# Summing four more steps of an attention pass as A (E - 1) g, with the rows of exp(0.2 s) made by ScalarE

## The chip, the core and the metric

The kernel runs on one core of a Trainium2 chip. The metric is the device time of one execution in microseconds (us); lower is better. The kernel before takes 2042.51 us in the median of three runs (2039.18 to 2042.93).

## What is computed

Two graph layers over 4096 nodes with 512 features, all in fp32. The adjacency A is a 4096 x 4096 matrix of zeros and ones, about 0.8% of it ones. Layer 0 has eight heads of 64 features:

```python
feats = einsum('nf,hfo->hno', X, W)
s_self = einsum('hno,ho->hn', feats, a_self)
s_neigh = einsum('hno,ho->hn', feats, a_neigh)
dense = s_self[:, :, None] + s_neigh[:, None, :]
dense = where(dense > 0, dense, 0.2 * dense)      # leaky
dense = dense * A[None, :, :]
attn = softmax(dense, axis=-1)                    # over all 4096, zeros too
out = einsum('hij,hjo->hio', attn, feats) + b
x = layernorm(x + relu(out))
```

Layer 1 is an attention within 32 graphs of 128 nodes each: query, key and value are x times Wq, Wk, Wv plus biases; the score within a graph is query · key · scale plus twice A; a softmax times the values is added to x and normalised. A second, general path in the file handles other inputs and does not run here.

## The kernel before

**Layer 0 without a score matrix.** exp of the leaky score is the larger of exp(s_self + s_neigh) and exp(0.2 (s_self + s_neigh)). Each of these is a product of something of the row i and something of the column j. So the kernel keeps, for each node and head, exponentials as columns (`d_all`, `e_all`, `e_b`) and as rows in DRAM (`pu_d`: rows p, u, and for some heads U = 1/u), and one VectorE operation makes a tile of weights: `q = max(p_row, d_j) * A` (L1534). ScalarE, and for every eighth tile VectorE, makes from `q` a mark of one byte that says which branch won (L1544, L1539); the marks summed by TensorE (`dens`, L1597) give the softmax's denominators.

**Passes, chunks, cycles, steps.** The heads are taken in four passes r of two heads. Each pass goes through four chunks c of 1024 nodes i, each chunk through 32 steps j of 128 neighbours. Passes 0 to 2 group eight steps to a cycle (`wide=8`), pass 3 four. TensorE's order is the program's (its schedule is written out by hand); the other engines' and the DMA queues' order is set by a scheduler at build time, except where `keep_in_program_order` pins an instruction. A step is:

- `accf += A f` with f split in two parts: four matmuls (L1558), which need no `q`;
- two `q`, one for each head, and their marks;
- `acc += q g`: eight matmuls of 32 columns, recorded as sixteen (L1581).

A cycle runs, on TensorE: L1558 of its steps, small pieces of other work, L1581 of its steps, then `dens` for eight steps. The chunk ends with `ys = (accf + S_col) * u_row + acc` on VectorE (L1278, L1286), whose transposes and denominators follow as pieces in later cycles.

**Folded steps.** Some steps are folded: VectorE makes `max(p_row, d_j) * U_row` (L1522) and then `(q - c_j) * A` (L1525), that is A (E - 1) g up to row and column factors; its L1581 matmuls go to `accf`, and the four L1558 matmuls of the step fall away. It needs the rows `U_row` (two of 512 KB) and the column `c_all`. Passes 0 and 3 have folded steps: pass 0 has j = 10, 18 in chunk 0 and j = 2, 10, 18 in the others; pass 3 has 6, 7 and 7 in chunks 1 to 3.

**Pass 0 has more to do.** It reads A itself as blocks of 1024 x 512 through the GpSimd queue (`a_b`, L605, three buffers, loaded ten steps ahead), turns them on TensorE (L617), casts them on ScalarE to `at` (L628), and stores `at` to DRAM (`at_d`, L629) for the later passes, which load it back (L635). It also sums the columns of exponentials over A (`ae`, L1479).

**Loads at SP.** At the start of each chunk: `p_row` (L1434, two of 512 KB, two buffers each) and `u_row` (L1440, two of 256 KB, one buffer). In each cycle: `f_s` (L1496, 512 KB for four steps) and `g_s` (L1501). `U_row` (L1462) goes into a buffer `ck` in pass 0. From pass 1 on, blocks `ck` of A are loaded and checked by ScalarE (L1249, L1250).

**Other work in pass 1.** `weights_of_layer_1` (L1018) is a generator. Each `yield` names a cost, and a cycle runs pieces until a credit of 6.0 is used up; pieces that end a chunk come first. It loads weights q, k and v (L1038), forms M = Wq^T Wk (L1043), turns v (L1055, L1056) and forms the bias terms with `partial_sums` (L572). M falls into the second to fourth cycle of chunk 2.

**Setup** (the first 160 us) forms the features (L818), and for each block k of four tiles the exponentials on ScalarE (L750, L751, L754); `rows_of_exponentials` (L778) takes reciprocals on VectorE (L780), turns them (L786), copies (L793) and stores the rows.

**Layer 1** (`layer_1`, L1088) runs its eight blocks as pieces in pass 3 and after it, with `values` (L1186, L1194) and `rows_out` (L1200, L1202).

Of the kernel before, what the change touches and what calls it, by code (L numbers as in the profile page):

```python
# [19 lines left out]
P = 128  # L20
# [384 lines left out]
def adjacency_streamed_path(  # L405
# [57 lines left out]
    f_d = dram.tile([PR, NT // 4, P, 4 * 2 * FP], F32, name="f_d")  # L463
    FOLDED = (0, PR - 1)
    FOLDS = {4: (1,), 5: (0, 1), 6: (0, 1, 2)}, {2: (1,), 4: (1,), 5: (0, 1), 6: (0, 1, 2)}
    HU = 2 * len(FOLDED)
    pu_d = dram.tile([2 * H + HU, N], F32, name="pu_d")
    at_d = dram.tile([NCH, NT, P, C], F32, name="at_d")
# [17 lines left out]
    for c in range(FC):  # L486
# [11 lines left out]
    nb_all = const.tile([P, NT, H], F32, name="nb_all")  # L498
    c_all = {
        r: (const if r else early).tile([P, NT, 2], F32, name="c_all") for r in FOLDED  # L500
    }
    below_0 = const.tile([P, 1], F32, name="below_0")
# [46 lines left out]
    def misc(shape, dtype=F32):  # L549

        banks.append(banks.pop(0))
        return banks[-1].tile(shape, dtype, name="ps_m")
# [86 lines left out]
    with tc.tile_pool(name="setup1", bufs=1, side="right") as one, tc.tile_pool(  # L639
# [60 lines left out]
        for c in range(FC // 2):  # L700
            score_columns(c, False)
        powers = one.tile([P, 5, H], F32, name="powers")
        for i, v in enumerate((ALPHA, 1.0, ALPHA - 1.0, 1.0 - ALPHA, -ALPHA)):
            nc.vector.memset(powers[:, i, :], v)
# [32 lines left out]
        def exponentials(k, u, sc):  # L737

            j = 4 * k + u
            if u == 0:  # L740
                pu_js[k] = two.tile([P, 4, 2 * H + HU], F32, name="pu_j")
            st = small.tile([P, 5, H], F32, name="st")
            for lo, hi, w in ((0, 3, 1), (3, 5, 0)):
                ends_of_setup["DVE", u] = nc.vector.tensor_tensor(
                    st[:, lo:hi].rearrange("p k (q h) -> p k q h", q=2),
                    sc[:, None, :, :, w].to_broadcast([P, hi - lo, 2, H // 2]),
                    powers[:, lo:hi].rearrange("p k (q h) -> p k q h", q=2),
                    OP.mult,
                )
            nc.scalar.activation(e_all[:, j], st[:, 0:2], AF.Exp)  # L750
            nc.scalar.activation(  # L751
                pu_js[k][:, u, : 2 * H].rearrange("p (k h) -> p k h", k=2), st[:, 3:5], AF.Exp
            )
            nc.scalar.activation(d_all[:, j, :], st[:, 2], AF.Exp)  # L754

        def parts_of_exponentials(k):
# [3 lines left out]
            )  # L760
            for r in FOLDED:
                nc.vector.reciprocal(
                    c_all[r][:, blk], e_all[:, blk, 1, 2 * r : 2 * r + 2]
                )
            eb = e_b[:, blk]
# [12 lines left out]
        def rows_of_exponentials(k):  # L778
            for i, r in enumerate(FOLDED):
                nc.vector.reciprocal(  # L780
                    pu_js[k][:, :, 2 * H + 2 * i : 2 * H + 2 * i + 2],
                    pu_js[k][:, :, H + 2 * r : H + 2 * r + 2],
                )
            pr = pss.tile([2 * H + HU, 4, P], F32, name="ps_set")
            for u in range(4):
                nc.tensor.transpose(pr[:, u, :], pu_js[k][:, u], ident)  # L786
            if k < NB - 1:
                row = late.tile([2 * H + HU, 4 * P], F32, name="pu_row")
            else:
                row = hp_.tile([P, CT, FP], F32, name="hst")  # L790
                row = row.rearrange("p t n -> p (t n)")[: 2 * H + HU, : 4 * P]
            rows[k] = row
            ends_of_setup["ROW"] = nc.scalar.copy(  # L793
                row.rearrange("p (q n k) -> p q k n", q=2, k=2),
                pr.rearrange("p (q k) n -> p q k n", q=2),
            )
            nc.gpsimd.dma_start(pu_d[:, ts(k, 4 * P)], row)
# [220 lines left out]
    def weights_of_layer_1(keep, wp):  # L1018
# [15 lines left out]
        ws = {}  # L1034
        for name, w in (("q", Wq), ("k", Wk), ("v", Wv)):
            yield 6.0
            ws[name] = wp.tile([P, FC, F], F32, name="w_" + name)
            nc.sync.dma_start(ws[name], w.rearrange("(c p) f -> p c f", p=P))  # L1038
        yield 6.0
        for m in range(FC):  # L1040
# [10 lines left out]
            yield 3.7  # L1051
        for o in range(FC):
            pv = misc([P, FC, P])
            for k in range(FC):
                nc.tensor.transpose(pv[:, k, :], ws["v"][:, o, ts(k, P)], ident)  # L1055
            nc.scalar.copy(L1["wvT"][:, :, ts(o, P)], pv)  # L1056
            if o % 2:
                yield 1.3

        pc = misc([P, 1])  # L1060
        kb = wp.tile([P, FC, P], F32, name="kb")
        nc.vector.tensor_copy(kb, cols["k"][:, :, None].to_broadcast([P, FC, P]))
# [5 lines left out]

        qb = ws["v"][:, 2, :P].rearrange("p (c n) -> p c n", c=FC)
        nc.vector.tensor_copy(qb, cols["q"][:, :, None].to_broadcast([P, FC, 32]))  # L1070
        pick = ws["v"][:, 3, :P]
        nc.vector.tensor_copy(pick, pick_col.to_broadcast([P, P]))
        parts = []
        for i, (wide, rhs) in enumerate(((kb, ws["q"]), (qb, ws["k"]))):
            pu = misc([P, F])
            partial_sums(pu, wide, rhs)
            parts.append(ws["v"][:, i, :])
            nc.scalar.mul(parts[i], pu, scale)
        yield 6.0
# [5 lines left out]
        nc.scalar.copy(L1["zb"], pz)  # L1085
        yield 2.0

    def layer_1(blk, x1b, lp, lp1, lp2):  # L1088
# [93 lines left out]

        def values(u):
            pv = misc([P, F])
            for f in range(FC):
                nc.tensor.matmul(  # L1186
# [5 lines left out]
                )  # L1192
            vs[u] = lp.tile([P, F], F32, name="v_t")
            nc.vector.tensor_add(vs[u], pv, L1["bv"])  # L1194

# [26 lines left out]
        values(2)  # L1222
        values(3)
        yield
        if blk == NT // 4 - 1:
            rows_out((2,))
            rows_out((3,))
        else:
            rows_out((2, 3))
        yield  # L1230
# [193 lines left out]
    steps = [(r, c, j) for r in range(PR) for c in range(NCH) for j in range(NT)]  # L1424

    def main_pass(r, ae=None, wide=4):

        for c in range(NCH):
            p_row = []
            for h in range(2):  # L1430
                p_row.append(rowp.tile([P, C], F32, name=f"p_row{h}"))
                in_order(
                    r == 0 and c < 2,
                    nc.sync.dma_start(p_row[h], broadcast_rows(pu_d[2 * r + h, ts(c, C)], P, C)),  # L1434
                )
            u_row = urowp.tile([P, C], F32, name="u_row")
            for h in range(2):
                in_order(
                    r == 0 and c < 2,
                    nc.sync.dma_start(  # L1440
                        u_row[h * FH : (h + 1) * FH, :],
                        broadcast_rows(pu_d[H + 2 * r + h, ts(c, C)], FH, C),
                    ),
                )
            U_row = []

            def folded(j):

                if r == PR - 1:
                    return r in FOLDED and c > 0 and j % 4 in FOLDS[c > 1].get(j // 4, ())  # L1450
                return r in FOLDED and j % 8 == 2 and (0 if c else 8) < j < NT - 8

            def rows_for_folded():

                for h in range(2):
                    if r == PR - 1:
                        pool, shape, name = ((hp_, [P, CT, FP], "hst"), (pools.get("lp1"), [P, C], "U_row"))[h]
                    else:
                        pool, shape, name = ckp, [P, CK], "ck"
# [3 lines left out]
                        U_row[h],  # L1463
                        broadcast_rows(pu_d[2 * H + 2 * FOLDED.index(r) + h, ts(c, C)], P, C),
                    )
# [24 lines left out]
            for j0 in range(0, NT, wide):  # L1490
# [3 lines left out]
                for k in range(j0 // 4, (j0 + wide) // 4):  # L1494
                    f_s[k] = fsp.tile([P, 4, 2, FP], F32R, name="f_s")
                    ins = nc.sync.dma_start(  # L1496
                        f_s[k].rearrange("p u s n -> p (u s n)").bitcast(F32), f_d[r, k]
                    )
# [4 lines left out]
                    )  # L1503
                    in_order(r == 0 and c == 0 and j0 < 16, ins)
                if at_step == 0:
                    cast_steps(0, 6, last_pair)
                if any(map(folded, range(NT))) and j0 == (4 if r else 0):
                    rows_for_folded()
# [126 lines left out]
    banks.extend([ctx.enter_context(tc.tile_pool(name="ps_misc2", bufs=2, space=PSUM))] * 2)  # L1635
    with tc.tile_pool(name="wl1", bufs=1, side="right") as wp:
        work.append(weights_of_layer_1(keep, wp))
        work.append(kind_of_graphs(wp))
# [69 lines left out]
```

## Time and profile before

| | us |
|---|---|
| runs, median (lowest to highest) | 2042.51 (2039.18 to 2042.93) |
| profiled execution, its own time | 2043.19 |
| its span, first to last instruction | 2041.3 |
| setup | 0 to 160.2 |
| pass 0 | 160.2 to 583.0 |
| pass 1 | 583.0 to 979.9 |
| pass 2 | 979.9 to 1355.5 |
| pass 3, with layer 1 beside it from its second chunk | 1355.5 to about 1902 |
| rest of layer 1 | to 2041.3 |

The stages are cut where TensorE starts the first L1558 matmul of a pass. A line of the profile's groups gives the line of the kernel, engine, operation, output and inputs, count, busy time and mean duration, and then the engine's idle time just before these instructions and what ended it. TensorE's recorded matmuls overlap, so their mean (594 ns for L1581) is longer than the distance between them; busy times of a group are the time covered. The granted TensorE clock is given as a share of full speed, the DMA share as the mean busy share of 16 engines (it can exceed 1, since packets overlap). Moved data is 558.7 MB, 274 GB/s in the mean.

### The profile page before, as it was taken

What the parts mean: (1) busy time and instruction counts of PE and PEld (TensorE: products, weight loads), DVE (VectorE), ACT (ScalarE), POOL (GpSimd) and SP (SyncE); (2) the same over time, 40 slices, a digit from 0 to 9 for tenths busy, and PEclk for the clock granted to TensorE, in tenths of its full rate; (3) what the DMA queues carried; (4) which work ended last, traced back from release to release, by engine and by line L of the source; (5) the groups of instructions that cost most, each with busy time, mean ns of one, the idle gap of its engine ahead of it and who ended that gap; (6) DMA issues with size and microseconds to landing.
All of it is one profiled execution on the core that took longest, in us unless ns stands there. A gap on an engine that the chain in (4) does not pass through costs nothing.

```text
span 2041.3 us, 38200 instructions
## 1 busy us (share of the span) xinstructions
PE 2005.9 (98%) x14981; PEld 1030.0 (50%) x14981; DVE 1744.8 (85%) x2219; ACT 1533.1 (75%) x1872; POOL 231.0 (11%) x362
## 2 busy tenths in 40 slices
PE   8999999999999999999999999999999999999997
PEld 7885545444444444444444544444444444445443
DVE  5668898898999998798999989999997897889754
ACT  3348988788888889788899889999786566567420
POOL 1222222222200000000000000000020210211111
PEclk9999999999999999999999999999999999999999
DMA  6899999999999999788999999989975775775211
GB/s 206 240 320 280 283 286 288 285 280 282 316 377 342 346 359 342 261 311 292 318 321 338 313 328 338 335 277 368 323 277 186 249 255 173 232 273 176 73 55 44
DMA packets 209386, 558.70 MB, mean 274 GB/s; under 512 B 25052, under 2 KB 66012, under 8 KB 209196
## 3 DMA queue, kind: packets, MB, share of 16 engines
q1 hardware_dynamic: 144844, 433.65, 61.0%
q0 software_dynamic: 62272, 121.98, 23.3%
q8 instruction: 120, 1.97, 0.4%
q10 hardware_dynamic: 2080, 0.52, 0.1%
q14 instruction: 70, 0.57, 0.1%
HBM read 499.13 MB, written 107.28 MB: 297 GB/s over the span
## 4 chain that ended last, share of the span: by engine, by line
PE 85%; DMA 7%; DVE 5%; issue 1%; ACT 1%; SPq 0%; POOL 0%; POOLq 0%; DVEq 0%; ACTq 0%
PE acc L1581 35%; PE accf L1558 20%; PE ps_fe L818 5%; PE ps_m L1186 5%; PE ps_m L1114 5%; PE dens L1597 5%; DMA a_b<-in_adj_dram 4%; DVE q L1534 3%; PE accf L1581 2%; PE ps_m L1141 1%; PE ps_m L1200 1%; DMA hp_l<-hs_d 1%; PE ps_m L617 1%; DMA at_d<-at 1%; PE ps_m L1043 1%
## 5 line engine op out<-in xcount | busy, mean ns | idle before, releaser
L1534 DVE SCALAR_TENSOR_TENSOR q<-p_row,d_all,at 128x1024 f32<-128x1024 f32 x962 | 1168.1, 1279 | 106.0 <-PE acc L1581 78.8
L1544 ACT ACTIVATE mark<-q,nb_all 128x1024 fp8e4<-128x1024 f32 x834 | 926.8, 1144 | 174.7 <-DVE q L1534 160.1
L1581 PE MATMUL acc<-q,g_s 128*32 128x512 f32 x7696 | 853.7, 594 | 1.1 <-DVE q L1534 0.4
L1581 PEld LDWEIGHTS acc<-q,g_s 128*32 128x32 f32 x7696 | 250.2, 110 | 557.2 <-issue 496.3
L1558 PE MATMUL accf<-at,f_s 128*128 128x512 f32 x1924 | 469.3, 400 | 1.7 <-ACT at L628 1.6
L1558 PEld LDWEIGHTS accf<-at,f_s 128*128 128x128 f32 x1924 | 357.2, 189 | 107.3 <-issue 27.8
L1249 ACT ACTIVATE ck<-ck,neg_half_f 128x1024 f32<-128x1024 f32 x128 | 146.0, 1141 | 28.5 <-DMA ck<-in_adj_dram 28.4
L1250 ACT ACTIVATE ck<-ck,neg_quarter 128x1024 f32<-128x1024 f32 x128 | 146.3, 1143 | 1.8
L1597 PE MATMUL dens<-mark,e_b 128*6 128x512 fp8e4 x2048 | 125.3, 379 | 2.5 <-DVE mark L1539 2.5
L818 PE MATMUL ps_fe<-w_sb_f,xT_f 128*128 128x264 f32 (+1 forms) x512 | 121.6, 395 | 1.7 <-ACT xT_f L730 1.7
L628 ACT CAST at<-ps_m 128x1024 fp32r<-128x1024 fp8e4 x124 | 116.3, 1022 | 4.8 <-issue 2.0
L1186 PE MATMUL ps_m<-wvT,x1T 128*128 128x512 f32 x256 | 114.2, 594 | 0.0
L1114 PE MATMUL ps_m<-x1T,M_sb 128*128 128x512 f32 x256 | 113.1, 595 | 0.0
L818 PEld LDWEIGHTS ps_fe<-w_sb_f,xT_f 128*128 128x128 f32 x512 | 100.5, 200 | 16.2 <-ACT xT_f L730 2.3
L1372 POOL DMA_DIRECT2D hs_d<-hst x12 | 10.7, 896 | 828.1 <-DVE hst L1362 817.5
L1539 DVE TENSOR_SCALAR mark<-q,d_all 128x1024 fp8e4<-128x1024 f32 x128 | 96.2, 751 | 4.7
L629 POOL DMA_DIRECT2D at_d<-at x128 | 69.1, 540 | 272.5 <-ACT at L628 94.0
L1597 PEld LDWEIGHTS <-e_b 128*6 128x6 bf16 x2048 | 55.9, 86 | 80.1 <-issue 38.2
L1529 ACT ACTIVATE mark<-q,below 128x1024 fp8e4<-128x1024 f32 x62 | 69.6, 1153 | 24.5 <-DVE q L1525 24.2
L1114 PEld LDWEIGHTS ps_m<-x1T,M_sb 128*128 128x128 f32 x256 | 48.0, 190 | 58.9 <-issue 57.1
L1525 DVE SCALAR_TENSOR_TENSOR q<-q,c_all,at 128x1024 f32<-128x1024 f32 x62 | 77.3, 1273 | 0.0
L1186 PEld LDWEIGHTS ps_m<-wvT,x1T 128*128 128x128 f32 x256 | 47.7, 190 | 56.3 <-issue 55.1
(207 smaller groups left out, 1294.9 us busy)
## 6 DMA issues: line engine op xcount, KB each, us to landing
at<-at_d SPq DMA_DIRECT2D x384, 512.0 KB, 6.1
f_s<-f_d SPq DMA_DIRECT2D x128, 512.0 KB, 7.8
at_d<-at POOLq DMA_DIRECT2D x128, 512.0 KB, 19.1
ck<-in_adj_dram SPq DMA_DIRECT2D x128, 512.0 KB, 5.5
g_s<-g_d SPq DMA_DIRECT2D x128, 256.0 KB, 5.9
f_d<-fst POOLq DMA_DIRECT2D x16, 1024.0 KB, 7.5
a_b<-in_adj_dram POOLq DMA_DIRECT2D x32, 512.0 KB, 21.7
p_row<-pu_d SPq DMA_DIRECT2D x32, 512.0 KB, 6.7
```

The costliest lines, as they stand in the source:

```text
L628: ends_of_setup["ACT"] = nc.scalar.copy(at, both[:, :, k])
L818: nc.tensor.matmul(pf[:, q, :, cols], tile_j(xTs[k][:, c].rearrange("p u n -> p (u n)"), u), w_sb[:, c, 4 * q : 4 * q + 4, cols], start=(c ...
L1114: nc.tensor.matmul(pz, L1["M"][:, f, ts(c, P)], x1T[:, f, :], start=(f == 0), stop=(f == FC - 1),)
L1186: nc.tensor.matmul(pv, x1T[:, f, ts(u, P)], L1["wvT"][:, f, :], start=(f == 0), stop=(f == FC - 1),)
L1249: tc.keep_in_program_order(nc.scalar.activation(ck, ck, AF.Square, bias=neg_half))
L1250: nc.scalar.activation(ck, ck, AF.Abs, bias=neg_quarter, accum_out=binp[:, k : k + 1])
L1534: ends_of_setup["Q"] = nc.vector.scalar_tensor_tensor(q, p_row[h], d_j, ats[r, c, j].bitcast(F32), op0=OP.max, op1=OP.mult)
L1539: nc.vector.tensor_scalar(mark, q, d_j, None, op0=OP.is_gt, saturate=False)
L1544: nc.scalar.activation(mark, q, AF.Sigmoid, bias=nb_all[:, j, hh : hh + 1], scale=BIG, saturate=False,)
L1558: nc.tensor.matmul(accf[:, s, :], f_s[j // 4][:, j % 4, w, :], ats[r, c, j][:, ts(s, HB)], start=(j == 0 and w == 0), stop=(j == NT - 1 an ...
L1581: nc.tensor.matmul(dst[o : o + 32, s, :], g_s[j // 4][:, j % 4, h, o % FH : o % FH + 32], qs[j, h][:, ts(s, HB)], start=(j == 0), stop=(j ...
L1597: nc.tensor.matmul(dens[lo : lo + 6, :], e_b[:, j, 2 * r + h, :], marks[j, h][:, ts(s, HB)], start=(j == 0), stop=(j == NT - 1),)
```

## The change

- ScalarE now makes the rows exp(0.2 s) directly, for all eight heads, beside the other two rows; the reciprocals L780 go, and `pu_d` has 24 rows and not 20. `c_all` is computed in setup for pass 0 alone; for passes 1 and 3 three VectorE operations at the pass's start add up the parts in `e_b` and take the reciprocal. These tiles lie in the pools `wl1` and `lp1`.
- Pass 0 folds j = 8, 16, 24 of every chunk. Pass 1 folds j = 8, 16, 24, 25 of chunk 2. Pass 3 folds the same steps as before.
- `f_s` loads only the steps from the first to the last that are not folded.
- In pass 0, `u_row` is loaded in the chunk's second cycle (chunk 0: at its start) and the next chunk's `p_row` in the third, both pinned.
- Weights v are loaded over weights q, after the sums that read weights q; their transposes come last in the generator. Two small tiles lie in `wvT` until it is written. The freed memory takes the rows `U_row` of pass 1.
- In the last block of layer 1 the last matmul of row 3's values comes after the product for row 2.

```diff
-    FOLDED = (0, PR - 1)
-    FOLDS = {4: (1,), 5: (0, 1), 6: (0, 1, 2)}, {2: (1,), 4: (1,), 5: (0, 1), 6: (0, 1, 2)}
-    pu_d = dram.tile([2 * H + HU, N], F32, name="pu_d")
+    FOLDED = (0, 1, PR - 1)
+    FOLDS = {1: {4: (1,), 5: (0, 1), 6: (0, 1, 2)}, 2: {2: (1,), 4: (1,), 5: (0, 1), 6: (0, 1, 2)}, 3: {2: (1,), 4: (1,), 5: (0, 1), 6: (0, 1, 2)}}
+    pu_d = dram.tile([3 * H, N], F32, name="pu_d")
...
-            nc.scalar.activation(
-                pu_js[k][:, u, : 2 * H].rearrange("p (k h) -> p k h", k=2), st[:, 3:5], AF.Exp
-            )
+            nc.scalar.activation(pu_js[k][:, u], st[:, 3:6], AF.Exp)
...
-            for i, r in enumerate(FOLDED):
-                nc.vector.reciprocal(
-                    pu_js[k][:, :, 2 * H + 2 * i : 2 * H + 2 * i + 2],
-                    pu_js[k][:, :, H + 2 * r : H + 2 * r + 2],
-                )
...
         ws = {}
-        for name, w in (("q", Wq), ("k", Wk), ("v", Wv)):
+        yield 6.0
+        for name, w in (("q", Wq), ("k", Wk)):
...
+        parts, sums = [], []
+        for wide, rhs in ((kb, ws["q"]), (qb, ws["k"])):
+            sums.append(misc([P, F]))
+            partial_sums(sums[-1], wide, rhs)
+        for i in range(2):
+            parts.append(ws["k"][:, i, :])
+            nc.scalar.mul(parts[i], sums[i], scale)
...
+        nc.sync.dma_start(ws["q"], Wv.rearrange("(c p) f -> p c f", p=P))
         yield 6.0
...
         values(2)
-        values(3)
-        yield
         if blk == NT // 4 - 1:
+            last = values(3, 3)
             rows_out((2,))
+            values(3, 3, last)
+            yield
             rows_out((3,))
...
+        if r in FOLDED and r:
+            c_all[r] = c_r = pools["lp1" if r == PR - 1 else "wl1"].tile(
+                [P, NT, 2], F32, name="c_all"
+            )
+            e_r = e_b[:, :, 2 * r : 2 * r + 2, 3:]
+            nc.vector.tensor_tensor(c_r, e_r[:, :, :, 0], e_r[:, :, :, 1], OP.add)
+            nc.vector.tensor_tensor(c_r, c_r, e_r[:, :, :, 2], OP.add)
+            nc.vector.reciprocal(c_r, c_r)
         for c in range(NCH):
...
+            p_row = p_rows.pop((r, c), None) or load_p_rows(r, c, (r, c) == (0, 0))
+            if r or c == 0:
+                u_row = load_u_row(r, c, r == 0)
...
-                return r in FOLDED and j % 8 == 2 and (0 if c else 8) < j < NT - 8
+                if r == 1:
+                    return c == 2 and j in (8, 16, 24, 25)
+                return r in FOLDED and j % 8 == 0 and j > 0
...
+                    live = [u for u in range(4) if not folded(4 * k + u)]
                     ins = nc.sync.dma_start(
-                        f_s[k].rearrange("p u s n -> p (u s n)").bitcast(F32), f_d[r, k]
+                        f_s[k][:, live[0] : live[-1] + 1].rearrange("p u s n -> p (u s n)").bitcast(F32),
+                        f_d[r, k, :, live[0] * 2 * FP : (live[-1] + 1) * 2 * FP],
                     )
...
+                if r == 0 and c and j0 == 8:
+                    u_row = load_u_row(r, c, True)
+                if r == 0 and c < NCH - 1 and j0 == 16:
+                    p_rows[r, c + 1] = load_p_rows(r, c + 1, True)
```

`load_p_rows` and `load_u_row` hold the same two DMA loops that stood at the chunk's start, with the pin as an argument.

## The prediction

> **What bounds the kernel now.** I read the page's busy shares first, then the table of stretches (one row per cycle of eight steps), the waits of TensorE, and TensorE's own order of time at the long waits. From the page:
>
> ```profile
> PE 2005.9 (98%) x14981; PEld 1030.0 (50%) x14981; DVE 1744.8 (85%) x2219; ACT 1533.1 (75%) x1872; POOL 231.0 (11%) x362
> ...
> L1534 DVE SCALAR_TENSOR_TENSOR q<-p_row,d_all,at 128x1024 f32<-128x1024 f32 x962 | 1168.1, 1279 | 106.0 <-PE acc L1581 78.8
> ```
>
> TensorE is busy for 98% of the span, so a step shortened on it counts; VectorE, with 85%, is next, and its largest idle time is spent waiting for TensorE to release `q`. The average hides the stages, so here are cycles of pass 0 and, in a second answer, the second to fourth cycle of pass 1's third chunk. The columns are the stretch, its length, then busy time of PE, PEld, DVE, ACT and POOL, the granted clock, the DMA share and GB/s.
>
> ```profile
> 343.60:369.40 25.80, 25.80 (x242) 13.13 (x241) 21.98 (x20) 23.30 (x23) 5.89 (x9) 1.00 1.09 303
> 369.40:401.35 31.95, 27.95 (x242) 12.44 (x242) 25.42 (x30) 24.70 (x25) 7.30 (x13) 0.95 1.12 259
> ...
> 478.70:507.56 28.86, 26.30 (x243) 12.50 (x242) 25.46 (x30) 24.55 (x25) 7.16 (x12) 1.00 1.12 265
> ...
> 559.18:583.04 23.86, 23.86 (x210) 10.73 (x208) 21.47 (x25) 18.15 (x18) 2.31 (x5) 1.00 1.03 381
> ```
>
> ```profile
> 794.48:822.39 27.91, 27.91 (x213) 13.73 (x213) 23.03 (x27) 24.44 (x28) 0.89 (x1) 1.00 0.92 329
> 822.39:848.97 26.58, 26.58 (x201) 12.46 (x201) 20.63 (x19) 21.52 (x25) 0.00 (x0) 1.00 0.76 253
> 848.97:878.95 29.98, 29.98 (x210) 13.98 (x209) 21.93 (x20) 22.41 (x27) 0.00 (x0) 1.00 0.84 259
> ```
>
> In pass 1 TensorE is never idle and VectorE has 4.9, 6.0 and 8.0 us to spare. In pass 0 the DMA engines have no idle share at all, and the first cycle of a chunk takes 28.9 and 32.0 us where its neighbours take about 25.8. TensorE's order of time shows why (start, duration, line, count, wait before it):
>
> ```profile
> 343.44 7.59 PE L1558 MATMUL accf<-at,f_s 128*128 128x512 f32 x32
> ...
> 369.24 7.01 PE L1558 MATMUL accf<-at,f_s 128*128 128x512 f32 x28
> 379.89 1.07 PE L617 MATMUL ps_m<-ident_b,a_b 128*128 128x128 bf16 x16 [3.63 <-DMA a_b<-in_adj_dram]
> 380.88 5.31 PE L1581 MATMUL acc<-q,g_s 128*32 128x512 f32 x32
> ```
>
> The adjacency block `a_b` comes late: 3.63 us of waiting, and then the same 32 matmuls that take 3.64 us elsewhere take 5.31. The three boundaries wait 0.41, 3.63 and 2.19 us; with the slow 1.67 that is 7.9 us.
>
> **The change part by part.**
>
> *A folded step.* It drops four of L1558's matmuls and sends L1581's to the other bank. Cycles with 28 of them take 6.67 us for that part, those with 32 take 7.59, so TensorE saves 0.93 us. VectorE gets two more operations; nine back to back take 10.85 us, 1.21 each, so 2.4 us.
>
> *Pass 1: four new folds* (j = 8, 16, 24, 25 of the third chunk). The three cycles shown become, on TensorE, 27.0, 25.7 and 28.1 us; on VectorE 25.4, 23.0 and 26.8. TensorE stays the longer in each. The idle time before VectorE's next `q` in these cycles is 3.6, 5.8 and 7.5 us, there because all eight `q` buffers are full; the second operation of a fold writes in place and takes no new buffer, so this time is usable. Gain 4 x 0.93 = **3.7 us**. The cover is thin in the last one (1.3 us); without it each fold there costs up to 1.5.
>
> *Pass 0: from 11 folds to 12, and from the third to the first step of a cycle.* Chunk 0 gains one: 0.9 us. In the other chunks a fold leaves the first cycle (VectorE 25.4 us, overloaded by `ys` and the reductions) for the fourth, where VectorE comes to 21.98 + 2.4 = 24.4 against TensorE's 24.9: covered. In the very last cycle it comes to 23.9 against 22.9: 0.95 us lost. Net **0**.
>
> *The loads of pass 0.* Between 352 and 364 us SP issues `u_row` (0.5 MB) and `p_row` (1.0 MB), just as the late `a_b` is issued (352.9, landed 379.8, wanted at 376.2). The change puts `u_row` into the second and `p_row` into the third cycle. The third carries 1.0 MB of `U_row` today (issued 318 and 427) with `a_b` landing in 22.6 to 23.3 us and no wait; `U_row` goes the other way, because its buffer is now in use until j = 24 and not 18. So a boundary sheds between 0.5 MB (if `U_row` falls wholly inside) and 1.5 MB: at the 303 GB/s of that cycle, 1.7 to 5.0 us. The waits then fall from 0.41, 3.63, 2.19 to 0, 1.9, 0.5 or to nothing, and the slow 1.67 us go with them (the wait of 2.19 us left the clock at 1.00): 5.5 to 7.9 us. Shorter `f_s` loads take away another 12 x 128 KB over the pass. Here the Trainium skill speaks against the change: "DMA: Bandwidth & Descriptors", section "Issuing engines are not separate DMA queues", says that transfers of all queues end up on the same 16 engines and interleave. By that, with a share of 1.0 to 1.1 in every cycle, a moved megabyte only makes another `a_b` late, and the gain is 0. The row of the third cycle says that the same megabyte there costs no wait. I follow the row, but not all the way: **6.0 us**.
>
> *Setup.* The two reciprocals of `rows_of_exponentials` (L780) go; the exponential on ScalarE gets 24 columns for 16, where the present 16 take 0.20 us on an engine busy 20 of 50 us: 0. TensorE waits twice for L780, 1.22 us each. At 43.77 nothing else is late (`pu_j` was ready at 40.8; TensorE is then busy without a gap until 156): between 0 and 1.2, I take **1.2**. At 157.94 the gain is 0, because the next matmul, at 160.17, waits for ScalarE, which works without a pause from 156.4 to 160.13. After that point the clock is at 0.50 to about 165, and 32 matmuls take 10.20 us where 7.5 is usual. "TensorE: Matmul & The Clock Gate", section "Why this matters for your kernels", asks for no idle gap over about 3 us; here gaps of 1.22 and 1.63, with 0.60 us of transposes between, were enough. By the letter of the rule the merged gap of 2.8 us would run at full clock and save 2.7; by the trace, the clock falls again. I keep the loss.
>
> *Small operations.* At the start of passes 1 and 3 VectorE computes `c_all` in three operations of 64 elements per partition; the nearest row (`z_all`, 128x64) takes 0.21 us, so 1.3 us in all, beside 22.6 of 23.6 us in pass 1. In pass 3 they write into `lp1`, memory that pass 2's extra buffers may still hold. Queued behind them on VectorE are the first `q`, for which TensorE waits: between 0 and about 3 us (VectorE's first eight `q` would start at 1353.6, when the last products of pass 2 end, and take 9.7, where TensorE wants the first at 1359.4). I take 0.3, as `x1b` goes through there today with a wait of 0.64.
>
> *Weights.* The load of weights v moves behind the sums that read weights q, so SP waits there for TensorE; behind it stand two `at`, the `ck` blocks and the next `f_s`. The sums (2.0 us) come straight after L1558, and then L1581's 13.9 us cover the loads: 0, and 2 us if not. The transposes move two cycles later, same length. U_row of pass 1 is loaded a cycle before its first use: 0.
>
> *The last block.* The product of row 2 goes ahead of the last matmul of row 3's values. Row 3's `v_t` (0.69 us) starts 0.9 later, but its statistics no longer queue behind row 2's last operation (ready at 2030.4, begun at 2031.28): between -0.3 and +0.3, taken 0.
>
> **Sum**, against the profiled execution's own 2043.19 us (span 2041.3): 1.2 + 6.0 + 3.7 - 0.3 = 10.6 us less, 2032.6. That execution lies 0.7 above the median of the runs, 2042.51, so **2032.0**.
>
> **The rivals.** Changes within 0.2% (4.1 us) can't be told from none; that is the bound below.
>
> *Transfers are the bound of pass 0.* The waits for `a_b` move to other cycles. For it: the DMA share and the rule; against it: the cycles that carry 1.0 MB without a wait. Then 1.2 + 3.7 - 0.3 = 4.6 remain: 2037.9, within 2036 to 2040, half on each side of the bound. Chance 0.25.
>
> *VectorE becomes the bound: slower.* If its idle time can't be used, each of the five added folds costs 2.4 us, and the boundary waits are covered by VectorE's own backlog, so their removal brings nothing: +12.0 - 1.2 + 0.3 = +11, 2053. It decides where VectorE's idle time in a cycle is under 2.4 us; it is 4.9 to 8.0 in the three cycles. Chance 0.05.
>
> *Better than forecast.* All 7.9 us of the boundaries go and the clock holds at the start of pass 0 (2.7): 15.2 less, 2027. Chance 0.12.
>
> The likeliest case, 2029 to 2035, has 0.58. Faster by over 0.2%: 0.58 + 0.12 + half of 0.25 = 0.82; within: 0.13; slower: 0.05. The range from 2026 to 2040 takes in all but the slower case and the outer ends.
>
> **What would show it.** In the changed profile: L1558 with 20 fewer matmuls, 62 + 10 = 72 marks in place of 62 from the folded steps; the three cycles of pass 1 at 27.0, 25.7 and 28.1 us without a wait of TensorE for `q`; the first cycles of pass 0's chunks at about 27 us, waits for `a_b` under 2 us and a clock of 1.00 there; no wait at 43.8. I am wrong if `a_b` is late in the second to fourth cycles, if the folds show TensorE's L1581 stretched, or if pass 3 starts with VectorE idle.

## The result and the profile after

The changed kernel takes 2029.1 us in the median of six runs (2026.69 to 2030.07), beside 2042.61 (2037.71 to 2045.53) in six for the kernel before: a ratio of 0.9937, 95% interval 0.9926 to 0.9948, so 0.6% faster and clear of the noise. Its profiled execution took 2029.65 us (span 2027.9), 13.5 less than the one of before. Cut by stages:

| stage | before | after | difference |
|---|---|---|---|
| setup | 160.17 | 156.42 | -3.75 |
| pass 0 | 422.80 | 415.67 | -7.13 |
| pass 1 | 396.90 | 394.97 | -1.93 |
| pass 2 | 375.60 | 375.62 | 0 |
| pass 3 and the rest of layer 1 | 685.8 | 685.2 | -0.6 |

The lines of the code have moved: L1558 is now L1584 (`accf`), L1581 is L1607 (`acc`), L1534 is L1560 (`q`), L617 is L614 (turning `a_b`), L628 is L625 (cast to `at`), L1525 is L1551 (second operation of a fold), and ScalarE's marks are L1570, those of folded steps L1555. From the page of the changed kernel, the engines, then two groups:

```profile
PE 1999.2 (99%) x14961; PEld 1023.0 (50%) x14961; DVE 1756.0 (87%) x2212; ACT 1524.7 (75%) x1872; POOL 231.2 (11%) x362
...
L1560 DVE SCALAR_TENSOR_TENSOR q<-p_row,d_all,at 128x1024 f32<-128x1024 f32 x952 | 1154.9, 1277 | 94.2 <-PE acc L1607 38.4
...
L1555 ACT ACTIVATE mark<-q,below 128x1024 fp8e4<-128x1024 f32 x72 | 81.6, 1145 | 78.4 <-DVE q L1551 77.9
```

TensorE runs 20 matmuls fewer in all, VectorE is busy 11 us longer, and there are 72 marks of folded steps. Now the stretches, with the columns as in the prediction: four cycles of pass 0 (the fourth of chunk 1, the first of chunk 2, the first of chunk 3 and the last) and the second to fourth cycle of pass 1's third chunk:

```profile
340.32:365.72 25.40, 25.20 (x241) 12.14 (x238) 23.10 (x21) 23.42 (x24) 7.30 (x11) 1.00 1.11 294
365.72:392.75 27.03, 26.67 (x248) 13.36 (x246) 24.18 (x29) 22.41 (x24) 6.63 (x10) 1.00 1.12 289
469.81:496.82 27.01, 26.66 (x249) 13.37 (x246) 24.46 (x29) 22.71 (x25) 6.78 (x10) 1.00 1.12 276
548.49:572.09 23.60, 23.41 (x208) 10.50 (x205) 23.04 (x27) 19.27 (x19) 2.31 (x5) 1.00 1.02 408
784.48:812.75 28.27, 27.18 (x212) 12.98 (x208) 25.24 (x29) 23.29 (x27) 0.89 (x1) 1.00 0.90 306
812.75:838.41 25.66, 25.66 (x200) 11.70 (x196) 23.03 (x21) 22.09 (x25) 0.00 (x0) 1.00 0.80 258
838.41:866.61 28.20, 28.20 (x205) 12.47 (x201) 25.43 (x23) 22.79 (x26) 0.00 (x0) 1.00 0.83 273
```

The first cycles of chunks 2 and 3 have fallen from 31.9 and 28.9 us to 27.0 at a clock of 1.00. Two of the pass 1 cycles gave what the folds promise (26.58 to 25.66, 29.98 to 28.20); the first did not (27.91 to 28.27): TensorE idles there for the first time. TensorE's order of time at the boundary that waited longest before:

```profile
364.84 1.07 PE L614 MATMUL ps_m<-ident_b,a_b 128*128 128x128 bf16 x16
365.72 7.60 PE L1584 MATMUL accf<-at,f_s 128*128 128x512 f32 x32
373.16 1.07 PE L614 MATMUL ps_m<-ident_b,a_b 128*128 128x128 bf16 x16
374.16 6.22 PE L1607 MATMUL acc<-q,g_s 128*32 128x512 f32 x56
```

No wait for `a_b` is left here or anywhere in pass 0, and the products that follow run at their usual pace. Pass 0 as a whole, before and after (the DMA share is the number before the last):

```profile
160.17:582.97 422.80, 415.47 (x3816) 204.62 (x3817) 380.94 (x393) 365.22 (x355) 97.26 (x158) 0.99 1.10 291
```

```profile
156.42:572.09 415.67, 412.24 (x3812) 202.43 (x3812) 383.09 (x395) 355.15 (x355) 98.87 (x158) 1.00 1.10 294
```

### The profile page after: what moved, and what is told of

It reads as the page before. It is cut to its first block, busy times and chain, and to the rows that moved or that the text cites. A ratio compares the mean times of both kernels' runs of the same rounds, so it can differ in the third digit from the quotient of the medians.

```text
span 2027.9 us, 38096 instructions
## 1 busy us (share of the span) xinstructions
PE 1999.2 (99%) x14961; PEld 1023.0 (50%) x14961; DVE 1756.0 (87%) x2212; ACT 1524.7 (75%) x1872; POOL 231.2 (11%) x362
## 5 line engine op out<-in xcount | busy, mean ns | idle before, releaser
L1560 DVE SCALAR_TENSOR_TENSOR q<-p_row,d_all,at 128x1024 f32<-128x1024 f32 x952 | 1154.9, 1277 | 94.2 <-PE acc L1607 38.4
L1570 ACT ACTIVATE mark<-q,nb_all 128x1024 fp8e4<-128x1024 f32 x824 | 907.6, 1148 | 137.9 <-DVE q L1560 126.9
L1607 PE MATMUL acc<-q,g_s 128*32 128x512 f32 x7616 | 841.9, 593 | 1.2 <-DVE q L1560 0.4
L1607 PEld LDWEIGHTS acc<-q,g_s 128*32 128x32 f32 x7616 | 248.5, 110 | 556.3 <-issue 495.5
L1584 PE MATMUL accf<-at,f_s 128*128 128x512 f32 x1904 | 464.3, 399 | 2.8 <-ACT at L625 2.7
L1584 PEld LDWEIGHTS accf<-at,f_s 128*128 128x128 f32 x1904 | 351.4, 189 | 109.2 <-issue 26.3
L1248 ACT ACTIVATE ck<-ck,neg_half_f 128x1024 f32<-128x1024 f32 x128 | 146.0, 1140 | 26.0 <-DMA ck<-in_adj_dram 25.7
L1555 ACT ACTIVATE mark<-q,below 128x1024 fp8e4<-128x1024 f32 x72 | 81.6, 1145 | 78.4 <-DVE q L1551 77.9
L625 ACT CAST at<-ps_m 128x1024 fp32r<-128x1024 fp8e4 x124 | 117.2, 1026 | 0.0
L1551 DVE SCALAR_TENSOR_TENSOR q<-q,c_all,at 128x1024 f32<-128x1024 f32 x72 | 90.5, 1274 | 0.0
```

Of the source, the lines that this page charges most:

```text
L625: ends_of_setup["ACT"] = nc.scalar.copy(at, both[:, :, k])
L1248: tc.keep_in_program_order(nc.scalar.activation(ck, ck, AF.Square, bias=neg_half))
L1560: ends_of_setup["Q"] = nc.vector.scalar_tensor_tensor(q, p_row[h], d_j, ats[r, c, j].bitcast(F32), op0=OP.max, op1=OP.mult)
L1570: nc.scalar.activation(mark, q, AF.Sigmoid, bias=nb_all[:, j, hh : hh + 1], scale=BIG, saturate=False,)
L1584: nc.tensor.matmul(accf[:, s, :], f_s[j // 4][:, j % 4, w, :], ats[r, c, j][:, ts(s, HB)], start=(j == 0 and w == 0), stop=(j == NT - 1 an ...
L1607: nc.tensor.matmul(dst[o : o + 32, s, :], g_s[j // 4][:, j % 4, h, o % FH : o % FH + 32], qs[j, h][:, ts(s, HB)], start=(j == 0), stop=(j ...
```

## The experiments

All runs in one table. The ratio is to the kernel before in the same job, with its 95% interval; stages and waits come from each kernel's one profiled execution, and waits may differ in another: e13's runs lie between 2028.78 and 2042.63.

| kernel | us, median (range) | ratio | setup | pass 0 | waits for a_b | pass 1 |
|---|---|---|---|---|---|---|
| before | 2042.61 (2037.71 to 2045.53) | | 160.2 | 422.8 | 6.2 in 3 | 396.9 |
| after | 2029.10 (2026.69 to 2030.07) | 0.9937 [0.9926, 0.9948] | 156.4 | 415.7 | 0 | 395.0 |
| e1 loads at the start | 2031.63 (2030.60 to 2034.13) | 0.9953 [0.9939, 0.9966] | 154.9 | 418.0 | 1.8 in 2 | 395.6 |
| e2 before + moved loads | 2039.21 (2034.74 to 2042.19) | 0.9986 [0.9976, 0.9996] | 156.9 | 419.9 | 3.8 in 2 | 396.9 |
| e3 no folds in pass 1 | 2033.21 (2031.73 to 2035.49) | 0.9958 [0.9945, 0.9972] | 156.3 | 415.7 | 0 | 398.1 |
| e4 no fold at step 8 of pass 1 | 2029.08 (2028.59 to 2031.27) | 0.9940 [0.9926, 0.9954] | 154.7 | 416.1 | 0 | 394.7 |
| e5 third step | 2037.80 (2033.00 to 2041.97) | 0.9981 [0.9969, 0.9993] | 158.4 | 423.4 | 5.4 in 2 | 395.0 |
| e6 last cycle unfolded | 2033.33 (2031.31 to 2035.04) | 0.9957 [0.9942, 0.9972] | 158.5 | 416.1 | 0 | 397.0 |
| e7 whole f_s | 2031.44 (2029.75 to 2038.39) | 0.9957 [0.9941, 0.9974] | 156.3 | 416.6 | 0.45 in 1 | 395.1 |
| e8 reciprocals back | 2034.69 (2031.24 to 2036.80) | 0.9966 [0.9954, 0.9978] | 158.0 | 417.5 | 0 | 395.1 |
| e10 fourth step | 2030.57 (2029.52 to 2035.07) | 0.9961 [0.9946, 0.9976] | 156.5 | 416.0 | 0 | 395.0 |
| e11 start, whole f_s | 2036.21 (2031.55 to 2041.31) | 0.9980 [0.9972, 0.9988] | 155.9 | 424.3 | 6.4 in 2 | 395.1 |
| e12 both repairs | 2030.18 (2027.38 to 2032.22) | 0.9955 [0.9940, 0.9969] | 156.6 | 416.2 | 0 | 393.8 |
| e13 third step, split f_s | 2032.34 (2028.78 to 2042.63) | 0.9963 [0.9955, 0.9970] | 156.3 | 420.6 | 3.6 in 1 | 393.7 |

**Is it the moved loads that freed the boundaries?** Two runs: the changed kernel with `p_row` and `u_row` at the chunk's start again, and the kernel before with these loads moved and nothing else.

```diff
-            p_row = p_rows.pop((r, c), None) or load_p_rows(r, c, (r, c) == (0, 0))
-            if r or c == 0:
-                u_row = load_u_row(r, c, r == 0)
+            p_row = load_p_rows(r, c, r == 0 and c < 2)
+            u_row = load_u_row(r, c, r == 0 and c < 2)
...
-                if r == 0 and c and j0 == 8:
-                    u_row = load_u_row(r, c, True)
-                if r == 0 and c < NCH - 1 and j0 == 16:
-                    p_rows[r, c + 1] = load_p_rows(r, c + 1, True)
```

> The changed kernel with one part undone: in pass 0 the rows p_row and u_row are loaded at the start of their chunk again. Theory (the waits at the chunk boundaries came from these 1.5 MB falling beside the late adjacency block): the waits of TensorE for a_b return at two or three boundaries, 3 to 8 us in pass 0, about 2034 us in all. Rival (the waits went because the fold left the first cycle of a chunk, or because less of f_s is loaded): pass 0 stays within 1 us of 415.7 us, about 2029 us.

> The kernel before with one part of the change alone: p_row and u_row of pass 0 are loaded in the third and second cycle of a chunk. Theory: the boundary waits go, pass 0 falls from 422.9 by 6 to 8 us, about 2035 us in all. Rival (the transfers are the bound, so a moved load only makes another block late; or the fold's place did it): pass 0 gains less than 2 us, about 2041 us.

With the loads at the start, the first cycles of chunks 2 and 3 grew by 0.7 and 1.4 us and pass 0 by 2.4, less than the 3 to 8 expected. In the kernel before, moving them alone made pass 0 3.0 us shorter: the three boundaries were at 26.4, 26.4 and 27.8 us, but one of the waits turned up two cycles on, in chunk 2's third cycle (30.6 us), where `U_row` and `p_row` (2 MB together, issued from 413.3 to 418.9) now both fall. TensorE there:

```profile
426.37 1.07 PE L617 MATMUL ps_m<-ident_b,a_b 128*128 128x128 bf16 x16 [2.68 <-DMA a_b<-in_adj_dram]
```

So the loads are part of the answer, and the rival that waits only move is partly right for the old places of the folds. Neither run explains the full 7 us of pass 0. At the boundary of chunk 3 the change does not even take `p_row` away: there the scheduler now issues the `p_row` of pass 1 (462.9 and 464.1 in the changed kernel), so that only the 0.5 MB of `u_row` left it, and the wait of 2.19 us still went.

**The other parts of pass 0's transfers.** In the changed kernel, `f_s` was loaded whole; then with both savings undone, which leaves only the new places of the folds.

```diff
-                        f_s[k][:, live[0] : live[-1] + 1].rearrange("p u s n -> p (u s n)").bitcast(F32),
-                        f_d[r, k, :, live[0] * 2 * FP : (live[-1] + 1) * 2 * FP],
+                        f_s[k].rearrange("p u s n -> p (u s n)").bitcast(F32),
+                        f_d[r, k],
```

> The changed kernel with f_s loaded whole in every cycle (1.6 MB more in pass 0). Theory (the waits for a_b went by the moved rows and by the chunk's first cycle being no longer folded, so that a_b is wanted 0.9 us later): pass 0 within 1 us of 415.7, 2029.5 in all. Rival (the load that fell away did it): waits for a_b come back, pass 0 3 us or more longer, 2032.

> As the changed kernel, but with both of its savings in pass 0's transfers undone: p_row and u_row at the chunk's start, and f_s always whole. What is left of the change in pass 0 are the places of the folds. If the parts add up (loads 2.4 us and f_s 1.0 in pass 0, each undone alone): pass 0 419 us, the program 2032 to 2034. If each of them alone was enough to keep a_b in time: waits for a_b of 5 to 8 us at the first cycles of chunks 2 and 3, pass 0 421 to 424, the program 2035 to 2039. If the places alone cured the boundaries: pass 0 416 to 417, the program 2030.

Whole `f_s` loads cost 1.0 us of pass 0, 0.9 of it in the first two cycles of chunk 3 (27.26 us for 27.01 and 26.20 for 25.55), where one wait of 0.45 us for `a_b` stands, at 504.19. Both savings undone cost 8.7, where the sum of the two alone is 3.3: the waits are back to 6.4 us, as before the change. The longer of the two:

```profile
376.62 1.07 PE L614 MATMUL ps_m<-ident_b,a_b 128*128 128x128 bf16 x16 [3.47 <-DMA a_b<-in_adj_dram]
```

So the parts do not add up. Each saving alone keeps most `a_b` in time, and the new places alone bring nothing. The runs agree for both together (e11, 0.9972 to 0.9988); either one alone (e1, e7) overlaps the changed kernel's interval, and its price is known from the profile only.

**The places of the folds.** Three runs. The first folds the third step (10, 18, 26), which keeps `f_s` whole; the second the fourth, with a short `f_s`; the third again the third step, with `f_s` loaded in two parts around the folded step (with the two small repairs told below).

```diff
-                return r in FOLDED and j % 8 == 0 and j > 0
+                return r in FOLDED and j % 8 == 2 and j > 8
```

> The changed kernel with the folded steps of pass 0 at j = 10, 18, 26 (third step of a cycle) in place of 8, 16, 24; f_s is then loaded whole in these cycles. Theory (a fold as the first step makes ScalarE stand behind its mark for 2.4 us, so the casts of at for the next steps come late and TensorE's accf part takes 7.0 us and not 6.7): the folded fourth cycles fall from 25.4 to 24.9 us and those of chunk 0 from 25.3 to 24.9, pass 0 by 2 us if no wait for a_b comes back, 2027 in all. Rival (the place in the cycle doesn't matter, VectorE's total does): pass 0 stays at 415.7.

> As the changed kernel, but pass 0 folds the fourth step of a cycle (11, 19, 27 of each chunk), so that the shortened f_s load is kept (128 KB less for each fold), as it was not with the third step. Theory, that the late a_b of the run with the third step came from the full f_s loads: the folded cycles take 24.9 us as there, waits for a_b stay under 2 us, pass 0 takes 411 to 413 us against 415.7, and the program 2025 to 2028. Rival, that they came from the place of U_row (its buffers are held two to three steps longer) and from the quicker cycles: waits for a_b of 4 to 6 us, pass 0 420 to 424, the program 2033 to 2039.

> As the kernel with both small repairs (no fold in the last cycle of pass 0, none at step 8 of pass 1), but pass 0 folds the third step of a cycle again, and f_s is loaded there in two parts around the folded step, so that the 128 KB are saved with this place too. If the full f_s loads were what made a_b late in the earlier run with the third step: no wait for a_b over 1 us, folded cycles 24.9 instead of 25.4, pass 0 414 us against 416.2, the program 2 us less than the kernel with both repairs. If the quicker cycles or the place itself (when U_row is released) made it late: waits for a_b of 3 to 5 us again, at the third cycle of chunk 2 and the first of chunk 3, pass 0 420 us or more, the program 4 us or more above the kernel with both repairs.

The third step has quicker cycles, 24.9 us in place of 25.4, as expected. ScalarE's order shows where the 0.5 come from. In the changed kernel TensorE begins the fourth cycle's L1584 at 340.32, and ScalarE stands in front of the casts that it needs:

```profile
340.17 1.15 ACT L1555 ACTIVATE mark<-q,below 128x1024 fp8e4<-128x1024 f32 x1 [2.38 <-DVE q L1551]
341.43 1.15 ACT L1570 ACTIVATE mark<-q,nb_all 128x1024 fp8e4<-128x1024 f32 x1
342.48 3.74 ACT L625 CAST at<-ps_m 128x1024 fp32r<-128x1024 fp8e4 x4
```

With the third step folded (e5) TensorE begins at 341.62, and one mark fewer stands there:

```profile
341.53 1.15 ACT L1570 ACTIVATE mark<-q,nb_all 128x1024 fp8e4<-128x1024 f32 x1 [1.24 <-DVE q L1560]
342.59 3.74 ACT L625 CAST at<-ps_m 128x1024 fp32r<-128x1024 fp8e4 x4
```

The casts start 2.2 us after L1584 in the one and 1.0 in the other; the 28 matmuls then take 7.2 us or 6.65. I had put this down to the folded mark itself. The fourth step (e10) corrects that: there the two marks in front are unfolded ones, the casts are as late (L1584 begins at 340.70), and the cycles are 25.4 too.

```profile
340.62 2.35 ACT L1570 ACTIVATE mark<-q,nb_all 128x1024 fp8e4<-128x1024 f32 x2 [1.24 <-DVE q L1560]
342.87 3.74 ACT L625 CAST at<-ps_m 128x1024 fp32r<-128x1024 fp8e4 x4
```

In these three kernels it is the number of marks ahead of the casts, each waiting for a `q` of VectorE, and not their kind.

But the quicker cycles bring nothing. With them `a_b` is late again, 5.4 us with whole `f_s`, and 3.6 with short ones:

```profile
479.14 1.89 PE L614 MATMUL ps_m<-ident_b,a_b 128*128 128x128 bf16 x16 [3.64 <-DMA a_b<-in_adj_dram]
```

So the theory that whole `f_s` loads alone made `a_b` late fails in e13. Pass 0 never got below 415.7 us: the profiled kernels with no wait for `a_b`, or with the 0.45 us of e7, take 415.7 to 417.5 us in it, those with longer waits 418 to 424, all with a DMA share of 1.10 over the whole pass and 122 to 124 MB moved.

What stays open is which property of the third step makes `a_b` late. The time at which `U_row` is released and loaded does not explain it by itself: counted from the start of chunk 2, `U_row` is issued 80 us on in e13, 83 in e5 and 82 in e10, which has no wait (73 in the changed kernel). What is left is the pace of the cycles, 24.9 us in e5 and e13 and 25.4 in e10, but no run changes the pace alone, and e13 has one more `f_s` load for each fold than e10.

**Pass 1.** Without its folds, and without the first of them alone.

```diff
-                    return c == 2 and j in (8, 16, 24, 25)
+                    return c == 2 and j in (16, 24, 25)
```

> The changed kernel without the four folded steps of pass 1. By the forecast's step (0.93 us for each fold) pass 1 gets 3.7 us longer, 398.7 us, and the whole 2032.8. By the trace of the changed kernel, where one of the four cycles got longer and not shorter, pass 1 gets 2.3 us longer (its cycles 2 to 4 of the third chunk 27.9, 26.6 and 30.0 us again, against 28.3, 25.7 and 28.2), and the whole 2031.4.

> The changed kernel with three folded steps in pass 1 (16, 24, 25), the one at j = 8 left out. Theory (the fold at j = 8 puts the reduction of the denominators behind VectorE's extra operations, and TensorE waits for the PSUM bank that it frees): the second cycle of the third chunk falls from 28.3 to 27.9 us although one fold less is done, the wait of 1.1 us is gone, the whole 2028.7. Rival (each fold is worth 0.9 us and the wait is an accident of this run): that cycle gets 0.5 to 0.9 us longer, the whole 2030.

Without any, the three cycles are back at 27.91, 26.58 and 30.01: the folds bring 2.4 us of the 3.7. The intervals of the runs, 0.9945 to 0.9972 without the folds and 0.9926 to 0.9948 with them, still touch. (Pass 1 is 3.1 longer; 0.7 of it lies in a cycle of chunk 0 that has no fold, and that is as long in e1, whose pass 1 is the changed kernel's.) The missing part is a new wait of the changed kernel, at the first product of M:

```profile
793.55 3.67 PE L1033 MATMUL ps_m<-w_k,w_q 128*128 128x512 f32 x8 [1.09 <-DVE parts L1337]
```

The bank of `ps_m` is freed by the reduction `parts`, which now stands behind VectorE's extra operations of step 8. Without that fold:

```profile
791.92 3.60 PE L1033 MATMUL ps_m<-w_k,w_q 128*128 128x512 f32 x8
```

The wait is gone and the cycle is at 27.90, 0.37 shorter than with a fold that should save 0.93. In the program's time that cannot be told from the changed kernel.

**The last cycle of pass 0.** The fold at step 24 of the last chunk taken out; then the same with the fold at step 8 of pass 1 gone and two copies of bias columns on GpSimd.

```diff
-                return r in FOLDED and j % 8 == 0 and j > 0
+                return r in FOLDED and j % 8 == 0 and 0 < j < (24 if c == NCH - 1 else NT)
```

> The changed kernel with the fold in the last cycle of pass 0 (j = 24 of the last chunk) left out. Theory (there VectorE is the bound: its 23.0 and 24.1 us in that cycle and the next are what they take): the two cycles take 47.1 us and not 47.8, 0.7 us less although one fold less is done, 2028.4 in all. Rival (TensorE is the bound): 0.9 us more, 2030.

> As the changed kernel, without the fold at step 24 of pass 0's last chunk and without the one at step 8 of pass 1, and with the two copies of bias columns (which stood among VectorE's first q of pass 1, waiting 2.89 us for a load, in the run without the last fold) on GpSimd. Theory, that VectorE's spill of the last fold costs 1.06 us in pass 1 and the fold itself saves 0.4: the last cycle of pass 0 takes 24.0 and the next 23.2 us (together 47.2 against 47.8), the cycle of step 8 27.9 against 28.3; together 1.0 us less than the changed kernel, 2028 us. Rival, that the next cycle is long for another reason (the first q of a pass): it stays at 24 us or more, and the program at 2029 to 2031.

The first of these missed both theories: the last cycle took 24.0 as expected, but the next one 26.2 where 23.1 or 24.2 stood to choose. VectorE shows an accident of the order that the scheduler chose:

```profile
576.06 6.07 DVE L1560 SCALAR_TENSOR_TENSOR q<-p_row,d_all,at 128x1024 f32<-128x1024 f32 x5
585.02 0.23 DVE L1052 COPY wvT<-b_q 128x128 f32<-128x128 f32 x1 [2.89 <-DMA b_q<-in_L_gnn_bq_dram]
```

The copy of a bias column of layer 1, which the change lets start at once as its place in `wvT` is free from the beginning, stood among the first `q` of pass 1 and waited 2.89 us for its load. In the changed kernel it runs at 603.1, ten microseconds after its load was issued, and waits for nothing. With the copies on GpSimd (e12) the two cycles take 24.0 and 23.12 us, 0.66 less than with the fold: the spill theory holds in the profile.

By this profile the two repairs take 1.0 us off the cycles that they concern and 0.6 off passes 0 and 1 together (810.06 for 810.64), but the runs (ratio 0.9955, 0.9940 to 0.9969) do not show it as better than the changed kernel (0.9926 to 0.9948). No run beat the changed kernel beyond its interval.

**The reciprocals.** Two reciprocals for each block put back in setup; their results overwrite what ScalarE made.

```diff
         def rows_of_exponentials(k):
+            for r in (0, PR - 1):
+                nc.vector.reciprocal(
+                    pu_js[k][:, :, 2, 2 * r : 2 * r + 2], pu_js[k][:, :, 1, 2 * r : 2 * r + 2]
+                )
```

> The changed kernel with two reciprocals for each block of the setup again, which overwrite the rows exp(0.2 s) of heads 0, 1, 6, 7. Theory: TensorE waits for them 1.2 us at the first block, and the last block ends 0.9 us later; setup up to the first accf matmul 2.1 us longer than in runs whose clock is full at 30 to 36 us (154.7 to 154.9), that is 156.8; 2031 in all. The forecast's step (1.2 us at the first block, nothing at the end): 155.9, 2030.3.

Setup got 1.6 us longer, at the same early clock as in the changed kernel's profile (0.57 from 30 to 34 us): between the 1.2 of the forecast's step and the 2.1 of the theory. Of it 1.23 lie at the wait for the reciprocal, now at 42.3, and 0.4 at the end. The rest of what this run cost, 1.7, lies in the first cycle of pass 0 (31.36 us for 29.66), and there it teaches more than it was made for. The changed kernel:

```profile
156.42 9.21 PE L1584 MATMUL accf<-at,f_s 128*128 128x512 f32 x32 [2.10 <-ACT at L625]
...
168.16 0.61 PE L614 MATMUL ps_m<-ident_b,a_b 128*128 128x128 bf16 x8 [1.63 <-DVE pu_all L794]
168.70 13.94 PE L1607 MATMUL acc<-q,g_s 128*32 128x512 f32 x128
```

With the reciprocals (the lines of the code lie four further down):

```profile
155.84 0.60 PE L777 MATMUL ps_set<-ident_f,pu_j 128*24 128x128 f32 x4 [0.58 <-DVE pu_j L772]
158.02 7.59 PE L1588 MATMUL accf<-at,f_s 128*128 128x512 f32 x32 [1.58 <-ACT at L625]
...
169.77 0.61 PE L614 MATMUL ps_m<-ident_b,a_b 128*128 128x128 bf16 x8 [3.26 <-DVE pu_all L798]
170.30 15.64 PE L1611 MATMUL acc<-q,g_s 128*32 128x512 f32 x128
```

Here the clock held: the 32 matmuls took 7.59 us and not 9.21. What was won was lost to a longer wait for VectorE's copy `pu_all`, and from the first matmul of `accf` to the first of `acc` it is 12.28 us in both. VectorE in the changed kernel over this stretch:

```profile
157.54 9.65 DVE L1560 SCALAR_TENSOR_TENSOR q<-p_row,d_all,at 128x1024 f32<-128x1024 f32 x8
167.22 0.75 DVE L1565 TENSOR_SCALAR mark<-q,d_all 128x1024 fp8e4<-128x1024 f32 x1
167.89 0.22 DVE L794 COPY pu_all<-ps_m 128x64 f32<-128x64 f32 x1
```

Eight `q`, a mark and then the copy: that chain ends the wait, whatever the clock. After the 3.26 us of idling the granted clock was 0.57 from 170 to 174 us, and the products took 15.64 us for 13.94.

## Why the prediction was right, and where its steps were off

The measured median lies 2.9 us below the forecast of 2032.0 and inside the stated range. The two large terms have the right cause in the main: late transfers at the boundaries of pass 0, of which the moved loads are one part, and TensorE's shorter work in pass 1. That the sum came so near is partly luck, since terms that were too small and too large offset each other. Step by step:

- **Setup, 1.2 forecast, 3.75 in the profile.** The wait at 43.8 is gone, as said. At the end the merged gap is 2.10 us where 1.22 and 1.63 stood with 0.60 of transposes between, and about 0.9 went (0.4 of it came back with the reciprocals in e8): "at 157.94 the gain is 0" was wrong, because I took ScalarE's order (four casts ahead of the first matmul that waits) as fixed, and the scheduler chose another. The rest, about 1.6, I take for no effect of the change: the clock between 30 and 38 us differs from one execution to the next. In e5 and e6, whose setup has the changed kernel's code, it was 0.50 from 30 to 34 us, as before the change, and setup ended at 158.4 and 158.5. The rows are before, after and e1, whose setup has the changed kernel's code (the granted clock is the third number from the end):

```profile
30.00:34.00 4.00, 4.00 (x11) 3.26 (x12) 3.38 (x13) 1.46 (x12) 0.50 (x1) 0.50 0.06 22
```

```profile
30.00:34.00 4.00, 4.00 (x13) 3.16 (x13) 3.72 (x13) 1.49 (x12) 0.81 (x1) 0.57 0.12 47
```

```profile
30.00:34.00 4.00, 4.00 (x22) 3.53 (x22) 3.59 (x13) 1.49 (x12) 0.67 (x1) 1.00 0.16 59
```

- **The clock at the start of pass 0, "I keep the loss".** It was lost again in the changed kernel (9.21 us), so the trace was the better guide than the rule about gaps. But the 2.7 us that followed from the rule, and that the rival "better" counted, were not there to win: e8 held the clock and gained nothing, since VectorE's first eight `q` set the time. That cycle became 0.8 us longer than before: all eight `q` now start after TensorE's first matmul, where one stood ahead of it, and `pu_all` waits behind them.
- **The boundary waits, 6.0 forecast.** All 7.9 us of waits and slow clock went. I followed the row of the third cycle "but not all the way"; the term was too small by 1.9. The row gave less than I read in it: 22.6 to 23.3 us are medians, and in the second of these cycles the two `a_b` beside `U_row` (issued 419.5 and 431.4) took 25.4 and 25.2 us to land. They were in time, but with little to spare, as e2 shows. The reason I gave was the moved loads alone. The runs say that they are not enough (3.0 in e2), that short `f_s` loads do nearly as well in their place (with the loads at the start, 1.8 us of waits in e1 and 6.4 in e11, where `f_s` is whole too), and that the two are not a sum: 2.4 and 1.0 us undone singly, 8.7 together. I had named the shorter `f_s` loads and counted them at nothing of their own.
- **The rule against it** (the Trainium skill, "DMA: Bandwidth & Descriptors", section "Issuing engines are not separate DMA queues": transfers of all queues run on the same 16 engines and interleave). The gain of 0 was my inference from it, with the share of 1.0 to 1.1; the section gives no price for a moved load. e2 shows a wait that moved with the megabyte, as inferred, while the changed kernel, with the same share of 1.10, lost all its waits. In e5 and e13, with their quicker cycles, waits are back.
- **Folds in pass 0, net 0 forecast, about +0.9.** Unfolding the three first cycles cost 0.42 each and not 0.93; I take VectorE to have held them before, busy for 25.4 us of each, but no run shows it. Folding the fourth cycles brought about 0.4 each where 0.93 was "covered": VectorE was not the limit, as I had checked, but ScalarE's casts were, which I had not looked at. Chunk 0 gained 0.3 after its first cycle for the 0.9 forecast. In the last cycle I expected a loss of 0.95; the cycle gained 0.4, and the loss came out in the next, the first of pass 1: 24.18 us for 23.12, with VectorE busy 24.07. e12 shows this as the fold's own: -0.66 without it.
- **Folds in pass 1, 3.7 forecast, 2.3.** Two cycles came out as forecast (25.66 and 28.20 for 25.7 and 28.1). In the first the step that failed is "this time is usable": I had compared sums of VectorE's time with TensorE's, and the idle time was there, but not ahead of `parts`, which TensorE's next bank waits for. e4 took that fold away, and the wait went.
- **Weights, small operations, the last block: 0, +0.3 and 0 forecast.** Two cycles of chunk 3 of pass 1, where the order of the weights' pieces changed, differ by +0.25 and -0.86. The stages after pass 2 are 0.6 shorter together, but the same code took from 682.7 (e11) to 685.7 us (e1) there, so this is no more than the spread of executions. I made no run for these terms, and what the last block brings stays open.

The sum in the profile: -3.75, -7.13, -1.93 and -0.6 make 13.4 of the 13.5 us. Of the 2.95 us of the profiled execution below the 2032.6 forecast for it, 1.6 are the early clock, which no forecast could hold; for the rest the terms that were too small (1.9 at the boundaries, 0.9 at the end of setup, about 1.5 in the weights, small operations and last block) and too large (1.4 and 0.9 in the folds of passes 1 and 0, 0.8 in the first cycle) left about 1.2. The rival "VectorE becomes the bound" never acted as a whole, but the spill into pass 1 and the wait for `parts` are of its kind, at 1.1 us each and not 2.4 for every fold.

## What to carry to other kernels

A stage whose transfer engines never rest can still shed all its waits if a few loads move away from a deadline or get shorter, but such savings need not add up: here each alone was nearly enough. Where nothing is late any more, look for the waits again after shortening compute steps: here quicker cycles came with late blocks. Before counting an engine's idle time as cover, look at which small instruction of it (a cast, a reduction that frees a bank, a copy) the critical engine waits for, and how many larger ones the change puts ahead of it; sums per cycle do not show that. A copy whose buffer becomes free earlier may be scheduled earlier too, ahead of work that cannot wait for its load.

## What was not expected of the hardware

- The granted clock of TensorE fell (0.57 in the mean of 156 to 160 us) after a single gap of 2.10 us at 154.3, but stayed at 1.00 after one of 3.47 us (e11, up to 376.62), and also after gaps of 0.58 and 1.58 us with 0.60 of transposes between (e8); before the change gaps of 1.22 and 1.63 had made it fall. After a gap of 3.26 us inside pass 0 (e8) it was 0.57 from 170 to 174 us, and the next 128 products took 1.70 us longer. By these figures the length of a gap alone does not say whether the clock falls.
- The clock between 30 and 38 us of the same instructions was 0.57 from 30 to 34 us in one profiled execution (after) and 1.00 in another (e1); setup ended at 156.4 and 154.9.
